# Two layers of a graph network and a mixture of experts: the first weights in two halves, and clears, a cast and filler matmuls moved at the start

## The chip, the cores and the metric

The kernel runs on one core of a Trainium2 chip. The metric is the device time of one launch in microseconds (us), the median of several runs. A profile is one further execution, taken by the hardware profiler; its times are counted from the start of its span.

## What is computed

x has 1250 rows of 1024 numbers; there are 40,000 edges, sorted by target. Everything is float32.

```python
def sage(h, W_self, W_neigh, b):        # twice, with a relu between
    agg = segment_sum(h[src], dst)      # sum over the edges that end in a row
    return h @ W_self + (agg * deg_inv[:, None]) @ W_neigh + b

x = x + sage2(relu(sage1(layernorm(x))))
t = layernorm(x)
logits = silu(t @ rw1 + rb1) @ rw2 + rb2          # 8 experts, the best 2 per row
w = softmax over the best 2
x = x + t + sum over experts of w[e] * (silu(t @ ew1[e] + eb1[e]) @ ew2[e] + eb2[e])
```

## The kernel before, in words

Rows go in ten blocks of 128 (the last has 98). The gather and sum over edges is done as a matrix product: a matrix C of counts (source row by target row, ten blocks of 128 x 1250) is built from one-hots, and a layer is C times (h times W_neigh), plus h times W_self. The kernel runs in stages: the start (rows in, layer norm, transposes into h0T), the self product of layer 1 with the counts in its gaps, the neighbour product and C times it, layer 2, the router, the experts.

The change lies in the start. What sets the order there:

- Loads (L150 to L159, L196). SyncE (SP) and ScalarE (ACT) each have a DMA queue. Blocks 0 and 1 of x come in two column halves each, one per queue (L153). Then SP loads the first quarter of W_self0, 1 MB, by `load_q` (L110), and blocks 4 and 5; ACT loads blocks 2 and 3 (L157) and src (L159), SP dst (L158). ACT also issues the load of the bias b0_p (L196), 1024 numbers of 4 bytes spread over 128 partitions, just after its first activation (L165), which also brings in the activation table. Blocks 6 to 9 are loaded later by `fetch_tokens` (L390), as the rows that they overwrite have been transposed. Each DMA raises a semaphore when it has landed; there are eight for these queues, taken in turn, so that a DMA waits on its queue until the one eight places earlier has landed.
- Clears of C (L356 to L365), before counts are added to it at L440. Ten blocks: 0, 1 and 5 to 7 by GpSimd (POOL), 2 and 3 by VectorE (DVE), 4 by ScalarE through `clear` (L363), 8 and 9 by ScalarE later, at L501.
- `layernorm_steps` (L311), a generator with three steps: statistics of the first half; statistics of the second half, their aggregate (L319) and the square root on ScalarE (L320); reciprocal (L322) and scaling (L323).
- The order written out by hand at L469 to L504 for VectorE, ScalarE and TensorE (`manual_schedule`): `pass_time` (L479) issues matmuls whose results nobody reads; `step` advances the layer norms of the blocks named; `turn_tokens` transposes a block on TensorE (L306) and copies it to h0T on ScalarE (L309); `self_unit` (L454) is one product of eight matmuls (L460) for a 128-column slice of the result and a chunk of rows, with the bias added on ScalarE (L464).
- `make_keys` (L209) works out each edge's place, `turn_keys` transposes the keys (L227, copied at L230), and after that the one-hots begin: `lane` (L189, a row 0 to 127 as float16, cast by `counted`, L186) is compared with the keys on POOL (L413) and ScalarE (L410, L411), `win` on VectorE (L418), and TensorE multiplies them (L421).
- `verdict` (L245) checks later whether this way of counting holds for the data; its first instruction is a memset of 960 numbers (L248).

What is not in the hand-written part is placed by a scheduler when the kernel is built; `keep_in_program_order` ties an instruction to its place in the program.

Of the kernel before, what the change touches and what calls it, by code (L numbers as in the profile page):

```python
# [12 lines left out]
F16 = mybir.dt.float16  # L13
# [8 lines left out]
P = 128  # L22
# [7 lines left out]
def kernel(  # L30
# [21 lines left out]
    nc = tc.nc  # L52
# [3 lines left out]
    KD = D // P  # L56
    KH = H // P
    HALF = D // 2
    QW = D // 4
# [14 lines left out]
    def blk(b):  # L74
        return slice(b * P, b * P + rows[b])
# [14 lines left out]
    WQ = KD * QW  # L90
# [3 lines left out]
    WW = L[:, NT + 4 * D :]  # L94

    def row_of(i):
        return SC[:, (i % 4) * D : (i % 4 + 1) * D]

    def first_row_of(i):

        return WW[:, WQ + (i - 4) * D : WQ + (i - 3) * D] if i in (4, 5) else row_of(i)

    turn = [0]

    def load_q(w, q):

        t = WW[:, turn[0] * WQ : (turn[0] + 1) * WQ].rearrange("p (k n) -> p k n", k=KD)
        turn[0] ^= 1
        tc.keep_in_program_order(
            nc.sync.dma_start(  # L110
                out=t, in_=w[:, q * QW : (q + 1) * QW].rearrange("(k p) n -> p k n", p=P)
            )
        )
        return t
# [35 lines left out]
    for b in range(2):  # L150
        for h, eng in enumerate((nc.sync, nc.scalar)):
            hs = slice(h * HALF, (h + 1) * HALF)
            eng.dma_start(out=row_of(b)[: rows[b], hs], in_=x[blk(b), hs])  # L153
    ws_first = load_q(w_self0, 0)
    for b in range(2, 6):
        eng = nc.scalar if b < 4 else nc.sync
        eng.dma_start(out=first_row_of(b)[: rows[b]], in_=x[blk(b), :])  # L157
    nc.sync.dma_start(out=dst_i, in_=dst.rearrange("(g n) -> g n", n=RE))  # L158
    nc.scalar.dma_start(out=src_i, in_=src.rearrange("(g n) -> g n", n=RE))  # L159
# [11 lines left out]
    def iota(shape, pattern, mult=0):  # L171

        n = 1
        for d in shape[1:]:
            n *= d
        ti = L[: shape[0], at_iota[0] : at_iota[0] + n].bitcast(I32)
        at_iota[0] += n
        assert at_iota[0] <= NT
        if len(shape) == 3:
            ti = ti.rearrange("p (a b) -> p a b", b=shape[2])  # L180
        nc.gpsimd.iota(ti, pattern=pattern, base=0, channel_multiplier=mult)
        return ti

    def counted(ti, name, dtype=F32):
        tf = const.tile(list(ti.shape), dtype, name=name)
        tc.keep_in_program_order(nc.vector.tensor_copy(tf, ti))  # L186
        return tf

    lane = counted(iota([P, P], [[1, P]]), "lane", F16)  # L189
    tiles_i = iota([P, NTILE], [[1, NTILE]])  # L190
    token_i = iota([P, NB], [[P, NB]], mult=1)
    own_row_i = iota([P, 1], [[0, 1]], mult=1)
# [6 lines left out]
    ext = base_i = keys = None  # L199
# [9 lines left out]
    def make_keys():  # L209

        nc.vector.tensor_reduce(ext[:, 0, :], dst_halves, AX.X, ALU.min)
        nc.vector.tensor_scalar(ext[:, 2, :], ext[:, 0, :], float(N - WIN), None, op0=ALU.min)
        nc.vector.tensor_scalar(hi_i, src_i, 7, None, op0=ALU.arith_shift_right)
        nc.vector.tensor_scalar(lo_i, src_i, P - 1, None, op0=ALU.bitwise_and)
        nc.vector.tensor_copy(hi_f, hi_i)
        nc.vector.tensor_copy(lo_f, lo_i)
        stt(key, hi_f, float(WIN), dst_f, op0=ALU.mult, op1=ALU.add)
        for i in range(2):
            part = key[:, i * EG : (i + 1) * EG]
            nc.vector.tensor_scalar(part, part, ext[:, 2, i : i + 1], None, op0=ALU.subtract)  # L220
# [11 lines left out]
    def turn_ranges():  # L232

        nc.vector.tensor_reduce(ext[:, 1, :], dst_halves, AX.X, ALU.max)
        for a in (2, 0, 1):
            pe = tpp.tile([P, 4, P], F32, name="tp")
            for i in range(2):
                nc.tensor.transpose(pe[:1, i, :R], ext[:, a, i : i + 1], ident[:R, :R])
            nc.vector.tensor_copy(
                gx[:, a, :].rearrange("o (r i) -> o i r", i=2), pe[:1, :2, :R]  # L240
            )
            if a == 2:
                nc.vector.tensor_copy(base_i, gx[:, 2, :])

    def verdict():  # L245

        bad = L[:1, 8480 : 8480 + 6 * NGR].rearrange("o (a g) -> o a g", a=6)
        nc.vector.memset(bad, -1.0)  # L248
        stt(bad[:, 0, :], hi_, float(1 - WIN), lo_, op0=ALU.add, op1=ALU.subtract)
        nc.vector.tensor_tensor(bad[:, 1, : NGR - 1], lo_[:, : NGR - 1], lo_[:, 1:], ALU.subtract)  # L250
        nc.vector.tensor_tensor(bad[:, 2, : NGR - 1], hi_[:, : NGR - 1], hi_[:, 1:], ALU.subtract)
        stt(
            bad[:, 3, : NGR - APART], hi_[:, : NGR - APART], 1.0, lo_[:, APART:],
            op0=ALU.add, op1=ALU.subtract,
        )
        nc.vector.tensor_scalar(bad[:, 4, :], hi_, float(1 - N), None, op0=ALU.add)
        nc.vector.tensor_scalar(bad[:, 5, :], lo_, -1.0, None, op0=ALU.mult)
        nc.vector.tensor_reduce(worst, bad.rearrange("o a g -> o (a g)"), AX.X, ALU.max)
        nc.vector.tensor_scalar(plain, worst, 0.0, None, op0=ALU.is_le)
# [51 lines left out]
    def layernorm_steps(o, t, m):  # L311

        st = small.tile([P, 2, 6], F32, name="st")
        mv = small.tile([P, 2], F32, name="mv")
        rs = small.tile([P, 1], F32, name="rs")
        nc.vector.bn_stats(st[:m, 0, :], t[:m, :HALF])
        yield
        nc.vector.bn_stats(st[:m, 1, :], t[:m, HALF:])
        nc.vector.bn_aggr(mv[:m], st[:m].rearrange("p a s -> p (a s)"))  # L319
        nc.scalar.activation(rs[:m], mv[:m, 1:2], AF.Sqrt, bias=eps[:m])  # L320
        yield
        nc.vector.reciprocal(rs[:m], rs[:m])  # L322
        nc.vector.tensor_scalar(  # L323
            o[:m], t[:m], mv[:m, 0:1], rs[:m], op0=ALU.subtract, op1=ALU.mult
        )
        yield
# [14 lines left out]
    def gnn_windows():  # L341
# [14 lines left out]
        for k in range(2):  # L356
            nc.gpsimd.memset(C[:, k, :].bitcast(F32), 0.0)
            nc.vector.memset(C[:, k + 2, :].bitcast(F32), 0.0)
        for k in range(5, 8):
            nc.gpsimd.memset(C[:, k, :].bitcast(F32), 0.0)  # L360

        def clear(k):
            nc.scalar.copy(C[:, k, :], none.to_broadcast([P, N]))  # L363

        clear(4)  # L365
        ones_r = cpool.tile([P, P], F32R, name="ones_r")
        nc.gpsimd.memset(ones_r.bitcast(F32), 1.0)

# [3 lines left out]

        yh = yp.tile([P, NB, QW], F32R, name="yh")
        yl = yp.tile([P, NB, QW], F32R, name="yl")
        nonlocal ext, base_i, keys
        ext = yp.tile([R, 3, 2], F32, name="ext")
        base_i = yp.tile([1, NGR], I32, name="base_i")

        keys = yp.tile([GP, 2, 2 * GC, R], F32, name="keys")
# [12 lines left out]
        def turn_tokens(b):  # L392
            put_transposed(h0T, 0, b, first_row_of(b), KD)
# [60 lines left out]
        def self_unit(w, d, c, halfway=None):  # L454
            c0, n = cchunks[c]
            ps = mm.tile([P, 512], F32, name="ps")
            for k in range(KD):
                if halfway is not None and k == KD // 2:
                    halfway()
                nc.tensor.matmul(  # L460
                    ps[:, :n], w[:, k, (d % 2) * P : (d % 2 + 1) * P], h0T[:, k, c0 : c0 + n],
                    start=(k == 0), stop=(k == KD - 1),
                )
            nc.scalar.activation(  # L464
                hT1[:, d, c0 : c0 + n], ps[:, :n], AF.Identity, bias=b0_p[:, d : d + 1]
            )


        with tc.manual_schedule(engines={ENG.DVE, ENG.Activation, ENG.PE}):  # L469
            norm = [layernorm_steps(first_row_of(b), first_row_of(b), P) for b in range(6)]  # L470

            def step(*bs):
                for b in bs:
                    next(norm[b])


            idle = mm.tile([P, 512], F32, name="ps")

            def pass_time(n):  # L479
                for _ in range(n):  # L480
                    nc.tensor.matmul(idle[:, :P], ident, ident, start=True, stop=True)

            pass_time(24)
            step(0, 0, 1, 0, 1)
            turn_tokens(0)
            step(1)
            turn_tokens(1)
            pass_time(4)
            step(2, 2, 3, 2, 3, 4, 3, 4)
            self_unit(ws_first, 0, 0)  # L490
            turn_tokens(2)
            step(5, 4, 5)
            self_unit(ws_first, 1, 0)
            step(5)
            turn_tokens(3)
            turn_tokens(4)
            turn_tokens(5)
            nc.vector.tensor_copy(dst_f, dst_i)
            make_keys()
            self_unit(ws_first, 0, 1, turn_keys)  # L500
            clear(8)  # L501
            clear(9)
            turn_ranges()
            self_unit(ws_first, 1, 1)  # L504
# [9 lines left out]
        some_groups(2)  # L514
        self_unit(ws_first, 1, 2)
        verdict()
        for q in range(1, 4):
            w_q = w_next
# [102 lines left out]
        for k in range(0, KB, 2):  # L621
            ks = slice(k, k + 2)
# [1100 lines left out]


    gnn_windows()
    ok = moe()
    with tc.If(ok == 0):
# [36 lines left out]
```

## Time and profile before

| | us |
|---|---|
| median of 3 runs | 1120.42 |
| lowest, highest | 1119.36, 6438.05 |
| the profiled execution | 1118.35 |
| its span, first to last instruction | 1116.6 |
| TensorE busy, of the span | 1089.5 (98%) |
| VectorE busy | 472.9 (42%) |
| POOL busy | 313.6 (28%) |
| ScalarE busy | 218.3 (20%) |

In a timeline a line has start, duration of the group, engine, line of the kernel, operation, what is written <- what is read, and in brackets the idle time of the engine before it with what ended it. SPq and ACTq are DMAs as they are issued on these queues, not their landing. In the chain of waits a line is start, length, and what the end of the kernel waited for in that stretch. In windows, after the stretch and its length, stand the busy times of TensorE, weight load, VectorE, ScalarE and POOL with the number of instructions, then TensorE's granted clock, the share of the 16 DMA engines and GB/s.

### The profile page before, as it was taken

To read this page: it belongs to the slowest core of one execution; us is meant where nothing else is said; L and a number is where in the kernel's file an instruction comes from. 1 tells how busy PE (TensorE), PEld (TensorE's weight loads), DVE (VectorE), ACT (ScalarE), POOL (GpSimd) and SP (SyncE) were. 2 spreads that over 40 slices of the span, in tenths; PEclk is the share of its full clock that TensorE was granted. 3 is DMA by queue.
4 is the path that set the end of the run, shared out by engine and by line. 5 is a ranking of instruction groups with operands and counts; after the bars stand their busy time and mean duration, and the time that the engine had idled before them with its cause. 6 is when DMAs were issued, how large, how long until landed. Compare 5 with 4: busy or idle time off the path is not lost.

```text
span 1116.6 us, 13639 instructions
## 1 busy us (share of the span) xinstructions
PE 1089.5 (98%) x4881; PEld 809.9 (73%) x4881; DVE 472.9 (42%) x1172; ACT 218.3 (20%) x511; POOL 313.6 (28%) x407
## 2 busy tenths in 40 slices
PE   8999999999999999999999999999999999999993
PEld 7556556888888888888888888887544577676761
DVE  8767777763121245342234142455522263222221
ACT  4522222101111101110010000023111133333331
POOL 2999898500000000022002211254000013232321
PEclk9999999999999999999999999999999999999997
DMA  8011011010100020033004270343960456677762
GB/s 260 12 39 40 1 38 39 2 38 1 38 1 1 1 76 19 1 114 126 22 1 154 96 269 7 105 171 147 334 207 1 160 180 180 183 182 192 192 172 47
DMA packets 62320, 107.37 MB, mean 96 GB/s; under 512 B 8906, under 2 KB 35690, under 8 KB 62240
## 3 DMA queue, kind: packets, MB, share of 16 engines
q1 hardware_dynamic: 51392, 79.69, 20.9%
q0 software_dynamic: 7056, 23.88, 9.2%
q10 hardware_dynamic: 3792, 2.79, 0.8%
q8 instruction: 43, 0.70, 0.3%
q14 instruction: 37, 0.30, 0.1%
HBM read 80.74 MB, written 27.42 MB: 97 GB/s over the span
## 4 chain that ended last, share of the span: by engine, by line
PE 74%; DMA 16%; DVE 4%; issue 3%; ACT 1%; POOL 1%; SPq 0%; POOLq 0%; ACTq 0%; DVEq 0%
DMA out_dram<-L 13%; PE ps L532 12%; PE ps L460 11%; PE psb L664 11%; PE ps L760 8%; PE ps L664 8%; PE ps L568 8%; PE ps L1230 4%; PE ps L1244 3%; PE cnt L421 3%; PE ps L1183 2%; DMA b_p<-in_L_gnn_b_dram 1%; DMA more<-in_L_gnn_W_self_dram 1%; DVE xw L140 1%; PE ps L1575 1%
## 5 line engine op out<-in xcount | busy, mean ns | idle before, releaser
L413 POOL TENSOR_SCALAR ol<-lane,keys 125x128 f16<-125x128 f16 x280 | 171.0, 628 | 31.8 <-ACT keys L230 22.3
L460 PE MATMUL ps<-h0T,L 128*128 128x498 f32 (+2 forms) x384 | 146.0, 514 | 0.2 <-ACT h0T L309 0.2
L532 PE MATMUL ps<-L,h0T 128*128 128x256 f32 (+1 forms) x640 | 142.2, 379 | 0.8 <-DVE yl L387 0.8
L756 POOL TENSOR_TENSOR L<-L 128x512 f32<-128x512 f32 (+1 forms) x20 | 28.2, 1417 | 393.5 <-DMA L<-in_x_dram 393.4
L532 PEld LDWEIGHTS ps<-L,h0T 128*128 128x128 f32 (+1 forms) x640 | 118.3, 187 | 19.0 <-DVE yl L387 1.1
L460 PEld LDWEIGHTS ps<-h0T,L 128*128 128x128 f32 x384 | 67.2, 190 | 38.7 <-issue 34.7
L418 DVE TENSOR_SCALAR oh<-win,keys 125x240 f16<-125x240 f16 x320 | 81.1, 307 | 29.7 <-PE cnt L421 28.0
L1575 PE MATMUL ps<-xw,L 128*128 x368 | 84.1, 380 | 0.7 <-issue 0.7
L1602 PE MATMUL ps<-xw,L 128*128 x184 | 82.8, 593 | 0.5 <-ACT L L1590 0.5
L568 PE MATMUL ps<-C,yh 128*128 128x256 f32 (+2 forms) x240 | 81.7, 355 | 0.0
L568 PE MATMUL ps<-C,yl 128*128 128x256 f32 (+2 forms) x240 | 81.4, 353 | 0.0
L760 PE MATMUL ps<-zh,C 128*128 128x512 f32 (+1 forms) x200 | 79.5, 398 | 0.0
L760 PE MATMUL ps<-zl,C 128*128 128x512 f32 (+1 forms) x200 | 78.6, 393 | 0.0
L1575 PEld LDWEIGHTS ps<-xw,L 128*128 128x128 f32 x368 | 68.0, 190 | 9.5 <-issue 1.4
L440 DVE TENSOR_TENSOR C<-C,cnt 128x240 f32 x160 | 64.4, 402 | 12.9 <-DVE C L440 1.3
L1608 POOL DMA_INDIRECT out_dram<-L x23 | 36.5, 1586 | 118.2 <-DVE L L1607 62.0
L1547 POOL DMA_INDIRECT L<-t_d,L x26 | 25.5, 980 | 143.7 <-DVE L L140 122.9
L1602 PEld LDWEIGHTS ps<-xw,L 128*128 128x128 f32 x184 | 34.9, 190 | 34.9 <-issue 32.3
L1607 DVE SCALAR_TENSOR_TENSOR L<-ps,L 128x512 f32<-128x512 f32 x46 | 34.5, 751 | 53.1 <-PE ps L1602 53.1
L664 PE MATMUL ps<-L 128*128 128x256 f32 x240 | 56.2, 379 | 0.0
L387 DVE TENSOR_TENSOR yl<-ps,yh 128x256 fp32r<-128x256 f32 (+1 forms) x40 | 16.9, 423 | 92.3 <-ACT yh L386 92.3
L421 PEld LDWEIGHTS <-ol 125*128 125x128 f16 x320 | 31.0, 97 | 34.3 <-POOL ol L413 16.5
(237 smaller groups left out, 1558.1 us busy)
## 6 DMA issues: line engine op xcount, KB each, us to landing
xw<-in_L_ffn_ew_dram SPq DMA_DIRECT2D x16, 1024.0 KB, 11.2
L<-in_L_ffn_eb_dram SPq DMA_DIRECT2D x23, 512.0 KB, 4.7
L<-in_x_dram SPq DMA_DIRECT2D x20, 256.0 KB, 2.6
v_d<-L SPq DMA_DIRECT2D x18, 256.0 KB, 2.0
xa<-v_d SPq DMA_DIRECT2D x18, 256.0 KB, 7.2
t_d<-L SPq DMA_DIRECT2D x9, 512.0 KB, 3.8
out_dram<-xa SPq DMA_DIRECT2D x9, 512.0 KB, 4.0
L<-in_L_gnn_W_self_dram SPq DMA_DIRECT2D x4, 1024.0 KB, 5.3
```

Source lines behind the costliest of these rows:

```text
L413: nc.gpsimd.tensor_scalar(ol[:, c, :], lane[:GP], k, None, op0=ALU.is_equal)
L418: nc.vector.tensor_scalar(oh, win[:GP], keys[:, 0, i * GC + c, r : r + 1], None, op0=ALU.is_equal)
L421: nc.tensor.matmul(ps[:, i, :GW], ol[:, i * GC + c, :], oh, start=(c == 0), stop=(c == GC - 1),)
L440: nc.vector.tensor_tensor(to, to.bitcast(F32), ps[:, i, :GW].rearrange("p (k w) -> p k w", k=NB), ALU.add,)
L460: nc.tensor.matmul(ps[:, :n], w[:, k, (d % 2) * P : (d % 2 + 1) * P], h0T[:, k, c0 : c0 + n], start=(k == 0), stop=(k == KD - 1),)
L532: nc.tensor.matmul(ps[:m, :QW], hT[:, k, blk(b)], w[:, k, :], start=(k == 0), stop=(k == KD - 1))
L568: nc.tensor.matmul(ps[:, :n], part[: rows[k], k, (d % 2) * P : (d % 2 + 1) * P], C[: rows[k], k, c0 : c0 + n], start=(k == 0 and part is y ...
L664: nc.tensor.matmul(ps, rows_of(k), w[:, k, :], start=(first and k == 0), stop=(k == KB - 1), skip_group_check=not first,)
L760: nc.tensor.matmul(ps[:m], C[: rows[k], k, blk(b)], part[: rows[k], k, :], start=(k == 0 and part is yh), stop=(k == NB - 1 and part is yl),)
L1230: nc.tensor.matmul(ps, a_[:, k, :], b_[:, k, :], start=(start and k == 0), stop=(stop and k == KB - 1),)
L1575: nc.tensor.matmul(ps[:, :H], xT[:, k, :], w1_all[:, ds(e, 1), k * H : (k + 1) * H], start=(k == 0), stop=(k == KD - 1),)
L1602: nc.tensor.matmul(ps, hT[:, q, :], w2_all[:, ds(e, 1), q * D + h * HALF : q * D + (h + 1) * HALF], start=(q == 0), stop=(q == KH - 1),)
```

## The change

- The first quarter of W_self0 is loaded in two halves of k (four of its eight 128-row blocks each), one on SP's queue and one on ACT's, in the place of one load on SP's queue.
- Of blocks 2 to 5 of x, even ones are on SP's queue and odd ones on ACT's; before, 2 and 3 were on ACT's, 4 and 5 on SP's.
- The cast of `lane` stands after `make_keys`, ahead of the transposes of the keys.
- The memset of the verdict is tied to its place in the program.
- Block 4 of C is cleared by POOL with 5 to 7, no longer by ScalarE.
- `pass_time` is 16 at the start, not 24, and 4 ahead of the first product are gone.

```diff
-    ws_first = load_q(w_self0, 0)
+
+    ws_first = WW[:, :WQ].rearrange("p (k n) -> p k n", k=KD)
+    turn[0] = 1
+    for h, eng in enumerate((nc.sync, nc.scalar)):
+        ks = slice(h * KD // 2, (h + 1) * KD // 2)
+        eng.dma_start(
+            out=ws_first[:, ks, :],
+            in_=w_self0[:, :QW].rearrange("(k p) n -> p k n", p=P)[:, ks, :],
+        )
     for b in range(2, 6):
-        eng = nc.scalar if b < 4 else nc.sync
+        eng = nc.scalar if b % 2 else nc.sync
         eng.dma_start(out=first_row_of(b)[: rows[b]], in_=x[blk(b), :])
...
-    lane = counted(iota([P, P], [[1, P]]), "lane", F16)
+    lane_i = iota([P, P], [[1, P]])
+    lane = None
...
-        nc.vector.memset(bad, -1.0)
+        tc.keep_in_program_order(nc.vector.memset(bad, -1.0))
...
-        for k in range(5, 8):
+        for k in range(4, 8):
             nc.gpsimd.memset(C[:, k, :].bitcast(F32), 0.0)
...
-        clear(4)
...
-            pass_time(24)
+            pass_time(16)
             step(0, 0, 1, 0, 1)
             turn_tokens(0)
             step(1)
             turn_tokens(1)
-            pass_time(4)
             step(2, 2, 3, 2, 3, 4, 3, 4)
...
             make_keys()
+            lane = counted(lane_i, "lane", F16)
             self_unit(ws_first, 0, 1, turn_keys)
```

The order in which the built program has ScalarE's instructions, with what each waits for in brackets, before and after:

```
before                                      after
x block 0, right half                       x block 0, right half
x block 1, right half                       x block 1, right half
x block 2                                   W_self0, second half of k
x block 3                                   x block 3
src [block 0, right half]                   x block 5 [block 0, right half]
table load                                  src [block 1, right half]
first activation                            table load
b0_p [block 1, right half]                  first activation
clear of C's block 4                        b0_p [W_self0, second half of k]
root of block 0                             root of block 0
```

More of the change, by code (lines that the diff above doesn't have):

```diff
@@ L374, in gnn_windows @@
         yl = yp.tile([P, NB, QW], F32R, name="yl")
-        nonlocal ext, base_i, keys
+        nonlocal ext, base_i, keys, lane
         ext = yp.tile([R, 3, 2], F32, name="ext")
```

## The prediction

> **What bounds the kernel now.** I read the page's busy shares first, then the chain of waits, then the timelines of ScalarE, VectorE and TensorE over the first 30 us, where every edit lies, and last the windows with the DMA rate.
>
> ```profile
> span 1116.6 us, 13639 instructions
> PE 1089.5 (98%) x4881; PEld 809.9 (73%) x4881; DVE 472.9 (42%) x1172; ACT 218.3 (20%) x511; POOL 313.6 (28%) x407
> ```
>
> TensorE leaves 27 us of 1116.6 idle. A change at the start can only move the point from which TensorE works without a break; what comes later keeps its length.
>
> ```profile
> 0.74 3.63 DMA L<-in_x_dram
> 5.81 13.03 DMA b_p<-in_L_gnn_b_dram
> 30.11 4.37 POOL ol L413 x4
> 34.94 6.72 PE ps L460 x16
> ```
>
> The chain of waits starts with rows of x, then follows one small transfer, the bias b0_p, issued on ScalarE's queue at 5.81 and landing at 18.84, and reaches TensorE, which then carries it. So two things set the start: block 0's way to TensorE, and the bias.
>
> ```profile
> 4.38 0.34 ACTq L159 DMA_DIRECT2D L<-in_src_dram  x1
> 4.75 1.28 ACT L165 ACT_TABLE_LOAD   x1 [4.75 <-DMA L<-in_x_dram]
> 5.81 0.40 ACTq L196 DMA_DIRECT2D b_p<-in_L_gnn_b_dram  x1
> 6.05 0.20 ACT L165 ACTIVATE rs<-eps 128x1 f32<-128x1 f32 x1
> 6.25 1.24 ACT L363 CAST C<-none 128x1250 fp32r<-128x1250 f32 x1
> 7.39 0.29 ACT L320 ACTIVATE rs<-mv,eps 128x1 f32<-128x1 f32 x1
> ```
>
> This is ScalarE. The order of instructions says which transfer each DMA on its queue waits for (a transfer takes over the semaphore of one eight places earlier): src waits for the second half of block 0, which lands at 4.36, and goes at 4.38; b0_p waits for the second half of block 1, which lands at 5.79, and goes at 5.81. The table load stands behind src and starts only at 4.75. A DMA that waits holds all of ScalarE behind it.
>
> ```profile
> 6.42 0.14 DVE L319 BATCH_NORM_AGGREGATE mv<-st 128x2 f32<-128x12 f32 x1
> 7.71 0.16 DVE L322 RECIPROCAL rs<-rs 128x1 f32<-128x1 f32 x1
> 7.91 0.81 DVE L323 TENSOR_SCALAR L<-L,mv,rs 128x1024 f32<-128x1024 f32 x1
> 8.78 1.09 PE L306 MATMUL tp<-ident,L 128*128 128x128 f32 x8 [0.22 <-DVE L L323]
> 11.05 1.07 PE L306 MATMUL tp<-ident,L 128*128 128x128 f32 x8 [1.17 <-ACT h0T L309]
> 12.84 3.62 PE L460 MATMUL ps<-h0T,L 128*128 128x256 f32 x16
> ```
>
> Block 0 goes root (7.39), reciprocal (7.71), scaling (7.91), transposes (8.78); block 1 follows 2.27 later by VectorE's fixed order; the first product starts at 12.84. From there to 34 us TensorE idles about 1.7 us in pieces, and from 35 to 430 hardly at all.
>
> **The change, part by part.** *Clear and casts.* Block 0's variance is there at 6.56, but its root waits until 7.39 for the 1.24 us clear of C's block 4 on ScalarE. The clear gone, it could run at 6.25: -1.14 if nothing takes its place. The memset of the verdict (0.86, at 5.63) and the lane cast (0.54, at 7.04) lie on VectorE before the reciprocal that waits for this root; they gain nothing more. Their new places: the memset among the counts near 51 us, where VectorE then waits 2.2 us for TensorE (0.86 if that cover went); the cast after the keys on VectorE, near 27.5, whose first readers, at 30 and later, wait for the keys' copies (0.54 if not). The clear as a fourth POOL memset: 3.33/3 = 1.11 us, ahead of the ones and the window iota (7.43), whose cast comes at 12.06; POOL then idles 22 us: 0 (1.11 if not). In all 0.
>
> *Filler.* 12 matmuls of 24 + 4 go. The first 8 end before 8.55, and the transposes wait for VectorE at 8.78; the last four end about when ScalarE's copy ends (11.71 + 1.07 = 12.78), and the product starts at 12.84: gain at most 0.06, taken as 0. The remaining 16 are 32 records: the trace has them start 213 ns apart to 4.5 us and 112 ns from there, so they end near 6.7.
>
> *ScalarE's queue, the term that decides.* It now holds block 0, block 1, half the weights, block 3, block 5, src, b0_p. One DMA more shifts whom each waits for: src now waits for block 1's half (5.79 instead of 4.36), so it goes at 5.81 to 6.15, the table load runs 6.18 to 7.46, the first activation to 7.68. b0_p now waits for the half of the weights on this queue, and behind b0_p stands block 0's root. When does that half land?
>
> ```profile
> 5.00:6.00 1.00, 1.00 (x11) 1.00 (x11) 0.86 (x2) 1.00 (x1) 1.00 (x2) 1.00 1.10 388
> 6.00:7.00 1.00, 1.00 (x11) 1.00 (x11) 1.00 (x3) 0.99 (x3) 1.00 (x2) 1.00 1.07 413
> 26.00:28.00 2.00, 2.00 (x6) 0.87 (x5) 2.00 (x7) 0.29 (x1) 0.00 (x0) 1.00 1.03 348
> ```
>
> The last number is GB/s. Two queues together moved 388 and 413; from 26 to 28 us one queue alone moved weights in 1 KB packets at 348. The Trainium skill (Trainium Kernel Development and Optimization, Key Constraints) speaks against the split: queues share the same 16 DMA engines, so a second one saves only time of issuing. Taken as a gain, the split would halve the weights' time to 0.5 MB / 0.36 = 1.5 us, landing near 7.3 and holding nothing (the table is loaded until 7.46). By the rule both halves run together: 1.05 MB at about 0.36 MB/us (1 KB packets) = 2.9 us from 5.2, when block 1's packets end, so 8.1, and 0.4 until the landing is reported (the spread of the landings in the trace is 0.3 to 0.6): 8.5. I take 8.5, since the windows show no sum above 413; ends 7.3 and 9.2. So b0_p goes at 8.5, takes 0.40, and the root starts at 8.94 instead of 7.39: **+1.55**.
>
> *Down to the product.* VectorE's order is fixed (block 1's second half stands behind block 0's scaling), so its chain moves whole: transposes of block 0 at 10.33, of block 1 at 12.60, product at 14.4. Blocks 2 and 3 had landed at 8.5 and 10.7, block 4 at 13.8; with the weights ahead, 2 and 3 land near 11.1 and 4 and 5 near 14; VectorE asks for block 2 at 12.4 and block 4 at 16.3. Hidden; if not, each us late is one lost on VectorE.
>
> *Bias.* It queues behind block 3, block 5 and src: 1.05 + 2.10 + 0.32 = 3.47 MB for both queues from 5.45 at 0.385 MB/us end at 14.5. Its 1024 packets of 4 B got some 125 per us beside 4 KB packets (12 to 17 us in the trace), 900 and more per us alone (rb1_p at 67 us). Blocks 8 and 9 (226 packets, 2.4 us) run beside it: some 300 packets, then 720 alone in 0.8: 17.7, reported near 18.3; bounds 16 and 14.5 + 1024/125 + 0.5 = 23.2. ScalarE asks for it after block 4's root, 17.52 + 1.55 = 19.1. So the stall that the page shows ("b_p", 1.40 us before L464) goes, but TensorE does not wait there: its second product runs until 20.79 + 1.55 = 22.3, and block 3's transposes need block 2's copies, over at 20.6. Nothing is won; nothing is lost while it lands before about 21.2.
>
> *Clock of TensorE.* From 6.7 to 10.3 it now idles 3.7 us. Row: an idle 1.17 us (9.87 to 11.05) left the 109 ns pace of transposes unchanged; after the last matmul, ending at 1100.19, the granted clock falls at 1103.60, 3.41 later. Rule: the Trainium skill (TensorE: Matmul & The Clock Gate, What's actually happening) says that a window of about 3.4 us spent idle halves the clock, and that the windows run freely. By the row nothing like it is shown in the middle of work: 0. By the rule a whole window lies in the gap with a chance of (3.7 - 3.4)/3.4 = 8%; then block 1's transposes (+0.8) and up to a further 1.2 us of products run at half pace: 0.8 to 2.0. I take 0.
>
> *Order of the counts.* From 34 to 230 us the schedule permutes counts and products; their number is the same. TensorE lost 1.1 us to POOL's one-hots in that stretch: bounds -0.5 and +1, taken as 0.
>
> *Sum.* -1.14 is not reached; 0 + 0 + 1.55 + 0 + 0 + 0 = +1.55. The profiled execution took 1118.35 (span 1116.6 + 1.75 around it), so 1119.9. The two ordinary runs shown, 1119.36 and 1120.42, lie 1.0 and 2.1 above it, mean 1.5: **1121.4**.
>
> **The rivals.**
> *A, the clock falls in the gap.* For: 3.7 against 3.41. Against: it barely fits. 1121.4 + 0.8 to 2.0 = 1122.2 to 1123.4.
> *B, the wait is short.* The weights' half lands before the table load is over; then the root starts at 7.68, +0.3: 1120.2. For: block 1's packets end a little earlier on SP's queue. Against: both halves share the engines.
> *C, the other side.* Nothing holds the root: the hardware lets it past the waiting DMAs, at 6.25, and TensorE works 1.14 earlier: 1118.7. It decides where the root starts before 7.39. Against: the table load waited 4.75 us behind src.
> *D, the bias is last again.* At 125 packets per us throughout it lands at 23.2, and block 2's copies with it; TensorE then stands up to 2 us at block 3, another 1 at blocks 4 and 5: up to 1124.4. It decides from a landing at 21.2.
>
> **How the numbers follow.** Forecast 0.55, A 0.13, B 0.12, C 0.10, D 0.10. Within the forecast, the landing (8.1 to 9.2) and the runs' own scatter of about 1 us give 1120 to 1122.8. The range leaves out half of C below (0.05 and the scatter's foot) and D's upper half with the scatter above: 1118.8 to 1124.2. The 2% about which a measurement of this kernel can tell from no change is 22 us, and no case reaches it: faster by more 0.01, within 0.98, slower by more 0.01.
>
> **What would show it.** The root of block 0 (L329 in the changed kernel) near 8.9, directly after the issue of b0_p near 8.5; the table load at 6.2; transposes of block 0 near 10.3; the first product near 14.4 at its old 3.6 us (longer: A); L472 without a wait for b_p (with one: D). The forecast is wrong if the root starts before 7.7, if b0_p goes with src, or if the shift at the first product is not there at 230 us.

## The result and the profile after

| | before | after |
|---|---|---|
| median of 20 runs each, us | 1119.07 | 1123.68 |
| lowest, highest, us | 1117.77, one run at 6438.05 | 1120.54, 1126.57 |
| ratio, 95% interval | | 1.0038, 1.0031 to 1.0045 |
| the profiled execution, us | 1118.35 | 1124.21 |
| its span, us | 1116.6 | 1122.4 |

The changed kernel is slower by 4.3 us (0.0038 of 1119). The forecast was 1121.4; the time lies inside the range of 1118.8 to 1124.2, near its upper end. It is a change of less than 2%, so "within 2%" came true; but its size is well measured, and it is nearly three times the +1.55 that the sum gave. Nothing here explains the one run at 6438.05; it moves neither the median nor the ratio.

The head of the page of the changed kernel:

```profile
span 1122.4 us, 13589 instructions
PE 1090.0 (97%) x4857; PEld 809.7 (72%) x4857; DVE 473.0 (42%) x1172; ACT 217.4 (19%) x510; POOL 313.7 (28%) x408
```

TensorE's busy time is the same within 0.5 us (1089.5 before); the span has grown by 5.8. So TensorE waits longer, and the chain of waits says where:

```profile
1.67 10.15 DMA L<-in_L_gnn_W_self_dram
...
11.85 0.40 ACTq L205
...
12.29 0.30 ACT rs L329
```

Before, the chain ran through the bias until 18.84. Now it starts with half of the first weights, issued on ScalarE's queue at 1.67 and landed at 11.82, then the issue of the bias, then block 0's root. The timeline of the changed kernel has the same stretch engine by engine:

```profile
5.85 0.34 ACTq L167 DMA_DIRECT2D L<-in_src_dram  x1
6.22 1.28 ACT L173 ACT_TABLE_LOAD   x1 [6.22 <-DMA L<-in_x_dram]
7.51 0.20 ACT L173 ACTIVATE rs<-eps 128x1 f32<-128x1 f32 x1
11.85 0.40 ACTq L205 DMA_DIRECT2D b_p<-in_L_gnn_b_dram  x1
12.29 0.29 ACT L329 ACTIVATE rs<-mv,eps 128x1 f32<-128x1 f32 x1 [4.58 <-DMA L<-in_L_gnn_W_self_dram]
12.82 0.81 DVE L332 TENSOR_SCALAR L<-L,mv,rs 128x1024 f32<-128x1024 f32 x1
13.69 1.97 PE L315 MATMUL tp<-ident,L 128*128 128x128 f32 x8 [5.47 <-DVE L L332]
17.71 3.74 PE L468 MATMUL ps<-h0T,L 128*128 128x256 f32 x16
```

ScalarE is ready at 7.71 and stands 4.58 us with nothing to do but wait for the weights' half. The root starts at 12.29 (7.39 before, +4.90), the first product at 17.71 (12.84 before, +4.87). The transposes take 1.97 in the place of 1.09, so the clock of TensorE has fallen too:

```profile
7.54:10.95 3.41, 0.67 (x6) 0.48 (x5) 0.00 (x0) 0.17 (x1) 1.33 (x3) 1.00 1.04 395
10.95:14.36 3.41, 0.67 (x3) 0.68 (x4) 1.67 (x4) 0.29 (x1) 0.00 (x0) 0.50 1.03 329
14.36:17.78 3.42, 3.12 (x16) 2.53 (x14) 2.99 (x8) 2.06 (x4) 0.00 (x0) 0.50 0.53 109
```

These are windows: the number before the DMA share is the granted clock, 0.50 from 10.95 to 17.78. What the start loses is carried on unchanged. The first matmul of three later stages, and the last matmul of all (us):

| | before | after | difference |
|---|---|---|---|
| first product (L460, L468 after) | 12.84 | 17.71 | +4.87 |
| its second run | 17.17 | 22.16 | +4.99 |
| product with C, layer 1 | 235.36 | 240.21 | +4.85 |
| product with C, layer 2 | 490.73 | 495.61 | +4.88 |
| last matmul | 1100.19 | 1106.05 | +5.86 |

The last microsecond comes in the router and expert stages. From the second product with C to the end the profile of before takes 609.5 us and that of after 610.4; those of the variants below whose granted clock does not fall there take 609.3 to 611.6, without order, so this is not put down to the change.

### The profile page after: what moved, and what is told of

Read it like the earlier page. It is cut to its first block, busy times and chain, and to the rows that moved or that the text cites. A ratio compares the mean times of both kernels' runs of the same rounds, so it can differ in the third digit from the quotient of the medians.

```text
span 1122.4 us, 13589 instructions
## 1 busy us (share of the span) xinstructions
PE 1090.0 (97%) x4857; PEld 809.7 (72%) x4857; DVE 473.0 (42%) x1172; ACT 217.4 (19%) x510; POOL 313.7 (28%) x408
## 4 chain that ended last, share of the span: by engine, by line
PE 75%; DMA 15%; issue 3%; DVE 3%; POOL 1%; ACT 1%; ACTq 0%; DVEq 0%; SPq 0%; POOLq 0%
PE ps L540 12%; DMA out_dram<-L 12%; PE ps L468 12%; PE psb L672 11%; PE ps L768 8%; PE ps L672 8%; PE ps L576 8%; PE ps L1238 4%; PE ps L1252 3%; PE cnt L429 3%; PE ps L1191 2%; DMA more<-in_L_gnn_W_self_dram 1%; DMA L<-in_L_gnn_W_self_dram 1%; PE tp L315 1%; DVE xw L140 1%
## 5 line engine op out<-in xcount | busy, mean ns | idle before, releaser
L468 PE MATMUL ps<-h0T,L 128*128 128x498 f32 (+2 forms) x384 | 147.0, 515 | 0.2 <-ACT h0T L318 0.2
L468 PEld LDWEIGHTS ps<-h0T,L 128*128 128x128 f32 x384 | 66.8, 190 | 38.7 <-issue 34.0
```

The source lines that it names most:

```text
L468: nc.tensor.matmul(ps[:, :n], w[:, k, (d % 2) * P : (d % 2 + 1) * P], h0T[:, k, c0 : c0 + n], start=(k == 0), stop=(k == KD - 1),)
```

## The experiments

My theory after the result: *the wait*. A DMA on ScalarE's queue that waits for an earlier one holds ScalarE, here for the weights' half; the half lands late because the two queues share the engines packet by packet. Rival *clock*: TensorE, idle for 5.5 us, fell to half pace, and that is the loss. Rival *rest*: clears, cast, memset and filler cost it. "The product with C" below is that of layer 1, which starts at 235.36 in the profile of before. "Before" and "after" below are the kernel before and the changed kernel; a ratio is always to the kernel before, with its 95% interval.

**1. After, with the bias on SP's queue.**

```diff
-    nc.scalar.dma_start(out=b0_p, ...)
+    nc.sync.dma_start(out=b0_p, ...)
```

> The changed kernel with one edit: the load of b0_p is issued on SP's queue, not on ScalarE's. Theory 1 (wait): block 0's root stands behind b0_p on ScalarE, which waits for ScalarE's half of the weights, landed at 11.82; without it the root follows the first activation, near 7.7, the transposes of block 0 start near 9.1, the first product between 12.5 and 13.1 (17.71 in the changed kernel, 12.84 before), and the time is that of before within 0.7 us, about 1119. Theory 2 (clock): TensorE's half clock from 10.95 to 17.78 costs the 4.6 us; it would go only as far as the idle gap goes. Theory 3 (bias late): b0_p, now behind dst, lands after 21.2 and the time stays above 1121.

Ratio 1.0008 (0.9997 to 1.0019), 14 runs. The timeline of this run:

```profile
7.67 0.28 ACT L329 ACTIVATE rs<-mv,eps 128x1 f32<-128x1 f32 x1
8.19 0.95 DVE L332 TENSOR_SCALAR L<-L,mv,rs 128x1024 f32<-128x1024 f32 x1
12.76 3.72 PE L468 MATMUL ps<-h0T,L 128*128 128x256 f32 x16 [0.24 <-ACT h0T L318]
```

The weights' half still lands late, at 11.50, and the bias still waits for it (issued at 11.52), but now on SP's queue, where no computing stands behind it. The root runs as soon as the first activation is over (7.67), and the product is back at 12.76. The product with C starts at 235.32. One word of the program takes back 0.0030 of the 0.0038, and the wait theory holds. The 0.9 us that are left lie a little above the 0.7 expected, and the interval includes none at all. They go with the granted clock: the four executions with a mean clock of 0.995 took 1118.8 us in the mean (fifteen of before with that clock 1118.5), the other ten 1121.1; in the profile it fell from 914.33 to 921.16.

**2. Before, with only the loads of the change** (the first hunk of the diff).

> The kernel before with the loads of the changed one alone (weights in two halves, rows of x even and odd); clears, cast, memset and filler as before. Theory 1 (wait): b0_p goes at 11.8, the clear of C's block 4 (1.24 us) and then the root stand behind it, root near 13.4, product near 18.7, time about 1125, that is 1 us above the changed kernel. Theory 2 (clock through less filler): with the 24 fillers the clock holds and the time is near 1120. If the clears and the cast were to blame: 1119.

Ratio 1.0051 (1.0034 to 1.0067), 6 runs. The timeline of this run:

```profile
10.86 0.40 ACTq L204 DMA_DIRECT2D b_p<-in_L_gnn_b_dram  x1
11.30 1.23 ACT L371 CAST C<-none 128x1250 fp32r<-128x1250 f32 x1 [3.59 <-DMA L<-in_L_gnn_W_self_dram]
12.44 0.29 ACT L328 ACTIVATE rs<-mv,eps 128x1 f32<-128x1 f32 x1
```

The half landed at 10.84; behind b0_p stood the old clear of C's block 4, and the root behind that. So the loads alone cost at least about as much as the whole change (the intervals overlap), and the rival *rest* falls. The first product came at 19.46, 6.62 late (the clock was 0.50 from 12.55 to 19.38), but the product with C only 5.06 late: here part of the loss was made up on the way.

**3. After, with the loads of before.**

```diff
-    for h, eng in enumerate((nc.sync, nc.scalar)):     # halves of k
+    ws_first = load_q(w_self0, 0)
...
-        eng = nc.scalar if b % 2 else nc.sync
+        eng = nc.scalar if b < 4 else nc.sync
```

> The changed kernel with the loads of before (one load of the weights on SP's queue, blocks 2 and 3 on ScalarE's); clears, cast, memset and filler as changed. Theory 1: the root runs at 6.3 (7.39 before), transposes of block 0 at 7.6, but the product waits for the weights, which land at 12.4 on that queue, and starts near 12.5 (12.84 before): time 1118.7, a gain of 0.4. If these edits brought their whole 1.14: 1117.9. Theory 2 (less filler costs clock): product longer than 3.6 us, time above 1120.

Ratio 1.0009 (0.9997 to 1.0021), 14 runs; the gain of 0.4 us that was expected is not seen. Here the root is early, at 6.27, as the missing clear allows. That gain is lost one instruction on:

```profile
4.03 4.41 POOL L361 MEMSET C<- 128x1250 f32 x4
6.27 0.29 ACT L321 ACTIVATE rs<-mv,eps 128x1 f32<-128x1 f32 x1
6.79 2.34 DVE L324 TENSOR_SCALAR L<-L,mv,rs 128x1024 f32<-128x1024 f32 x1
9.19 1.09 PE L307 MATMUL tp<-ident,L 128*128 128x128 f32 x8 [1.13 <-DVE L L324]
```

VectorE's scaling, 0.81 elsewhere, takes 2.34 us. POOL's four clears last until about 8.4 (4.03 + 4.41; its next instruction starts at 8.36), and 8.36 + 0.81 = 9.17, about when the scaling ends (9.13): it was held until they were over. Run 6, with one clear less, tests this. The Trainium skill (SBUF — State Buffer, SBUF: two separate sides) says that VectorE and GpSimd share a pair of ports under an exclusive lock, held for a whole instruction. This row agrees and gives it a price, 1.5 us: the scaling stood behind what was left of the third clear and the whole of the fourth. VectorE's statistics beside the same clears took their usual 0.7, so not every instruction is held. In the profile the clock fell too, from 201.78 to 205.19, and the product with C came 1.43 late.

**4. After, with more filler (38), so that TensorE doesn't idle.**

```diff
-            pass_time(16)
+            pass_time(38)
```

> The changed kernel with 38 fillers in place of 16, so that TensorE is busy until about 11 to 13 us and its clock does not fall. Theory 1 (wait): the root stays at 12.3, block 0's transposes take 1.1 us in place of 2.0, block 1's too, and the product starts 0.5 us earlier, near 17.1; time about 1123. Theory 2 (clock): the 4.6 us come back, time about 1119.5.

Ratio 1.0047 (1.0029 to 1.0064), 6 runs. The granted clock stayed at 1.00 at the start (from 6.93 to 204.90), and nothing was won:

```profile
11.31 0.29 ACT L329 ACTIVATE rs<-mv,eps 128x1 f32<-128x1 f32 x1 [2.99 <-DMA L<-in_L_gnn_W_self_dram]
12.71 1.09 PE L315 MATMUL tp<-ident,L 128*128 128x128 f32 x8
16.28 3.72 PE L468 MATMUL ps<-h0T,L 128*128 128x256 f32 x16 [0.24 <-ACT h0T L318]
```

The half landed at 10.85, and the product is 3.44 late at an unbroken clock; a fall from 204.90 to 208.31 came later, and the product with C is 4.88 late. The rival *clock* falls as the cause of the 4 us. What the clock cost in after is seen in the distance from root to product: 5.42 in after, 4.97 here, so 0.45 us.

**5. After, with the weights parted 5 to 3 blocks of k,** the smaller part on ScalarE's queue.

```diff
-        ks = slice(h * KD // 2, (h + 1) * KD // 2)
+        ks = slice(5, KD) if h else slice(0, 5)
```

> The changed kernel with the weights split five to three (640 packets of 1 KB on SP's queue, 384 on ScalarE's) in place of four to four. Theory (queues share by packet, and once SP's weights are through its packets are 4 KB): ScalarE's part is through before SP's, near 7.8 to 8.3, so b0_p goes at 8.3, the root of block 0 near 8.8 in place of 12.3, the product near 13.9, time about 1120.3. If ScalarE's queue is slow for another reason, its part lands after 10.5 and the time stays above 1122.

Ratio 1.0039 (1.0027 to 1.0050), 6 runs: no gain, though the wait became shorter as the theory says. The timeline of this run:

```profile
8.69 0.40 ACTq L205 DMA_DIRECT2D b_p<-in_L_gnn_b_dram  x1
9.13 0.29 ACT L329 ACTIVATE rs<-mv,eps 128x1 f32<-128x1 f32 x1 [1.30 <-DMA L<-in_L_gnn_W_self_dram]
14.55 5.51 PE L468 MATMUL ps<-h0T,L 128*128 128x256 f32 x16
```

The part landed at 8.66 and the product started at 14.55, 3.16 earlier than in after. But it ran for 5.51 us in the place of 3.6: the clock was 0.50 from 11.39 to 18.22, and the second product came 6.23 after the first (4.33 before). The fall, which cost little in after because TensorE had nothing to do then, hit full work here. The profile's product with C is 3.08 late.

**6. As 3, with C's block 4 cleared by ScalarE between later roots,** three clears on POOL.

```diff
-        for k in range(4, 8):
+        for k in range(5, 8):
...
-            step(2, 2, 3, 2, 3, 4, 3, 4)
+            step(2, 2, 3, 2)
+            clear(4)
+            step(3, 4, 3, 4)
```

> The run with the loads of before and the other edits (e3_old_loads), with one edit: block 4 of C is cleared by ScalarE again, between the roots of blocks 2 and 3, and POOL has three clears after the first two, not four. Theory (POOL's clears hold VectorE's scaling): POOL ends its clears at 7.36 in place of 8.44, and the scaling of block 0, which took 2.34 us from 6.79 to 9.13, ends near 8.0; transposes of block 0 at 8.1 (9.19), product at 12.4 when the weights have landed, time 1118.5 to 1119. If POOL has nothing to do with it, the scaling still ends at 9.1.

Ratio 1.0012 (1.0003 to 1.0021), 10 runs: slower than before, where the same or a small gain was expected. With POOL free sooner, the scaling takes 1.03, and block 0's transposes start at 8.10, against 8.78 before. Then:

```profile
12.80 5.38 PE L460 MATMUL ps<-h0T,L 128*128 128x256 f32 x16 [1.38 <-DMA L<-in_L_gnn_W_self_dram]
```

TensorE waits 1.38 us for the first weights, which in this order of loads land at 12.66 (12.42 in before). The clock, 0.50 from 13.30 to 16.71, then made the product 5.38 long in the place of 3.6, and the product with C came 1.15 late. An earlier block 0 alone can win at most 0.4 us: in the kernel before, the first product at 12.84 already stood just behind its weights.

**7. Bias on SP's queue, table loaded first, weights 5 to 3, blocks 4 and 7 of C cleared by ScalarE between later roots.**

> The changed kernel with what the runs point to: b0_p on SP's queue, the table load ahead of every DMA that waits, weights five to three, clears of C's blocks 4 and 7 by ScalarE between the roots of blocks 2, 3 and 4, so that POOL ends its clears at 6.25. Theory: root near 6.1, scaling over at 7.5, transposes of block 0 at 7.6 (8.78 before), the product near 11.2 (12.84 before): time 1.0 to 1.6 us below before, 1117.3 to 1118. If block 3's rows, late behind the weights (13.2), hold VectorE, half of that goes.

Ratio 1.0019 (1.0009 to 1.0029), 12 runs. A gain of 1.0 to 1.6 us was expected. The product starts at 11.01, 1.83 earlier than before, but then:

```profile
12.53 0.69 DVE L324 BATCH_NORM_STATS2 st<-L 128x6 f32<-128x512 f32 x1 [2.93 <-DMA L<-in_x_dram]
```

VectorE waits for block 2's rows, which land at 12.50, and the second product comes at 16.63, only 0.54 earlier. By the product with C the profile is 0.63 behind. What the weights win, the rows lose.

**8. After, with blocks 2 to 5 all on ScalarE's queue,** so that no rows compete with the weights' half from SP's queue.

```diff
-        eng = nc.scalar if b % 2 else nc.sync
+        eng = nc.scalar
```

> The changed kernel with blocks 2 to 5 all on ScalarE's queue behind its half of the weights, so that SP's queue has only dst behind its own half and no 4 KB packets run beside the weights. Theory (4 KB packets of SP's queue took the rate from ScalarE's half): the half lands near 8.6, as forecast, in place of 11.82; root near 9.1, product near 14.2, time about 1120.8. If the half is late for another reason it lands after 10.5.

Ratio 1.0036 (1.0022 to 1.0051), 4 runs. The timeline of this run:

```profile
9.89 0.40 ACTq L205 DMA_DIRECT2D b_p<-in_L_gnn_b_dram  x1
10.34 0.29 ACT L329 ACTIVATE rs<-mv,eps 128x1 f32<-128x1 f32 x1 [2.13 <-DMA L<-in_L_gnn_W_self_dram]
```

The half landed at 9.87 in the place of 11.82: the rows of the other queue held it back by 1 to 2 us (10.84 to 11.82 in the profiles where they run beside it). But 8.6 was expected, and 9.87 lies between that and the 10.5 of the rival: the rows are a large part of the delay and not all of it. The clock fell twice (10.15 to 16.98 and 204.71 to 208.12), and the product with C was 4.53 late.

**9. As 5, with filler (28, and the 4 back),** to keep the clock up.

```diff
-            pass_time(16)
+            pass_time(28)
...
+            pass_time(4)
             step(2, 2, 3, 2, 3, 4, 3, 4)
```

> The changed kernel with the weights parted 5 to 3 blocks of k, as before in one run, but with TensorE's filler made longer (28 at the start, and the 4 ahead of the first product back), so that it doesn't idle while the root waits. Theory (the landing of ScalarE's part holds the root, and in the 5:3 run the fallen clock took back what the earlier landing gave): root 9.1, transposes of block 0 at 10.5, first product 14.1 to 14.6, no half clock before 25 us, second product 4.4 later at 18.5 to 19, ratio to the kernel before 1.0010 to 1.0020. Rival (the clock was not what took it back): the second product again 6.2 after the first, or the ratio stays at 1.0039.

Ratio 1.0039 (1.0027 to 1.0051), 12 runs from 1120.99 to 1126.39: above what was expected, and the same 1.0039 as without the filler, which was one sign of the rival. The other sign did not come: in the profile the clock stayed up, and the second product came 4.33 after the first:

```profile
10.12 0.29 ACT L329 ACTIVATE rs<-mv,eps 128x1 f32<-128x1 f32 x1 [2.41 <-DMA L<-in_L_gnn_W_self_dram]
15.57 3.62 PE L468 MATMUL ps<-h0T,L 128*128 128x256 f32 x16
```

But the same part of the weights landed at 9.65, not at 8.66: 15 of the 16 DMA engines had reported by 8.72, the last one 0.93 later, and the wait is for all. The profile lost 2.8 us (root +2.73, product +2.73, product with C +2.80). The timed runs lost 4.4, and the clock of each run tells them apart: five with a mean granted clock of 0.994 or more took 1121.3 us in the mean, 2.3 above the runs of before at such a clock, and the seven below it 1124.1. Why it falls in more runs here than in before, and where, was not seen in a profile and stays open.

**10. Three blocks of rows first.** Blocks 0, 1 and 2 in halves on both queues ahead of the weights' halves, the table first, bias and src on SP's queue, clears of C's blocks 4 and 7 between later roots, filler 14 and 2.

> Blocks 0, 1 and 2 of x in halves on both queues ahead of the weights' two halves, the table loaded first, the bias on SP's queue, the clears of C's blocks 4 and 7 on ScalarE between later roots. Theory (what is left of the start is the rows' and the weights' arrival, and a change there is carried to the end one to one): root 6.0 to 6.3, first product 11.0 to 12.5, no wait of VectorE for block 2, second product 15.5 to 17, time 0.5 to 1.6 us below the kernel before (ratio 0.9986 to 0.9996). Rival (the engines' sum of bytes sets it, so a row that comes earlier makes the weights late by as much): the first product waits for weights until 12.8 or later and the ratio is 1.000 to 1.002.

Ratio 1.0001 (0.9991 to 1.0011), 12 runs. The root was expected at 6.0 to 6.3 and came at 7.70:

```profile
4.34 3.32 ACTq L168 DMA_DIRECT2D L<-in_x_dram  x2
7.70 0.29 ACT L328 ACTIVATE rs<-mv,eps 128x1 f32<-128x1 f32 x1 [4.06 <-DMA L<-in_x_dram]
```

The first line holds the issues of blocks 3 and 5. Block 5's takes over the semaphore of block 2's right half, waits until that lands at 7.30, and the root stands behind it: the same mechanism again, with another transfer, that I had built in without seeing it. The first product came at 13.95, not at 11.0 to 12.5: the weights had landed at 11.31, so it did not wait for them as the rival had it, but the late root and a clock of 0.50 from 11.05 to 14.46 held it. The ratio is the rival's.

**11. As 1, with the filler of before (24 and 4).**

> The changed kernel with the bias on SP's queue and the filler of the kernel before (24 and 4). If the 0.0008 that the run with the bias alone on SP's queue stayed above the kernel before came from the clock falling at the start for want of filler: ratio 0.9997 to 1.0003. If it comes from the changed order of the counts near 200 us: 1.0005 to 1.0012, with the half clock near 201 to 208 in the profile. First product 12.8 to 13.1 either way.

Ratio 1.0019 (1.0005 to 1.0033), 12 runs; the point lies above both of the narrow bands that were expected, and the interval overlaps that of run 1. The filler is no help. Block 1's transposes start at 11.44 (11.45 in run 1), but the first product at 13.24 (12.76): 0.48 later, because the four matmuls of `pass_time(4)` still run when the copy that the product waits for is over:

```profile
12.34 1.06 PE L489 MATMUL ps<-ident 128*128 128x128 f32 x8
13.24 3.62 PE L468 MATMUL ps<-h0T,L 128*128 128x256 f32 x16
```

**12. As 10, with block 5 on SP's queue.**

```diff
-        eng = nc.scalar if b % 2 else nc.sync
+        eng = nc.scalar if b < 4 else nc.sync
```

> As the run with three blocks of rows first, but block 5 goes on SP's queue instead of ScalarE's. In that run block 5's transfer stood ahead of block 0's root on ScalarE's queue, waited there for block 2's right half (landed 7.3) and kept the root until 7.70. Theory (a transfer that waits on ScalarE's queue holds what stands behind it): the root at 6.0 to 6.3, transposes of block 0 at 7.5 to 8, those of block 1 at 9.7 to 10.2, first product 11.3 to 12.0 (it needs block 1's first copy and the weights, which landed at 11.3), second product 15.6 to 16.6, C's product 0.5 to 1.5 us earlier than in the kernel before, ratio 0.9980 to 0.9995. Rival (the root waited for something else): root again after 7.5, ratio 0.9993 to 1.001.

Ratio 1.0001 (0.9989 to 1.0014), 12 runs. Of the timeline:

```profile
5.81 0.29 ACT L328 ACTIVATE rs<-mv,eps 128x1 f32<-128x1 f32 x1 [2.17 <-DVE mv L327]
10.91 3.68 PE L467 MATMUL ps<-h0T,L 128*128 128x256 f32 x16
14.18 0.69 DVE L324 BATCH_NORM_STATS2 st<-L 128x6 f32<-128x512 f32 x1 [3.28 <-DMA L<-in_x_dram]
16.08 1.06 PE L314 MATMUL tp<-ident,L 128*128 128x128 f32 x8 [1.49 <-issue]
```

The root comes 1.89 earlier than in run 10, for a transfer moved from one queue to the other, and the first product starts at 10.91, 1.93 ahead of before. But block 3's rows land only at 14.16; VectorE waits 3.28 us for them, and in its fixed order block 2's scaling stands behind (15.16). TensorE waits for that, the second product comes at 16.98 (17.17 before), and at the product with C the profile is 0.78 behind. The theory of the root is right and the forecast of a gain wrong: rows and first weights together fill the DMA engines until about 14 us (their share in windows of 2 us is 0.93 to 1.10 from 2 to 14), and in the orders tried here one of them was always late. None of the twelve was faster than the kernel before.

## Why the prediction was right and wrong

**The mechanism was right.** Two queues, one more DMA, so b0_p waits for the weights' half and holds the root: run 1 against after, and run 12 against run 10, show it, each with one transfer moved to the other queue and no other edit. The table load was to start at 6.2 and did (6.22). The shift was to be whole at 230 us, and it is (+4.87 at the first product, +4.85 at 235). The bias was not to be late, and L472 has no wait for it; it landed at 16.11, earlier than the 18.3 worked out.

**The size was wrong in one term,** the landing of ScalarE's half: 8.5 in the sum, with ends 7.3 and 9.2, and 11.82 in the profile (10.84 to 11.82 in five profiles with this order of loads). Packets of the two queues in the changed kernel that ended in each half microsecond, counted in the trace (those of 4 bytes left out):

```
from us    SP's queue                     ScalarE's queue
5.0        103 x 1 KB, 4 x 2 KB           43 x 2 KB
5.5        148 x 1 KB                     41 x 1 KB
6.0         95 x 1 KB                     88 x 1 KB
6.5         85 x 1 KB                     87 x 1 KB
7.0         61 x 1 KB, 6 x 4 KB           79 x 1 KB
7.5         20 x 1 KB, 24 x 4 KB          52 x 1 KB
8.0         38 x 4 KB                     36 x 1 KB
8.5         41 x 4 KB                     45 x 1 KB
9.0         33 x 4 KB                     43 x 1 KB
9.5         40 x 4 KB                     20 x 1 KB, 5 x 4 KB
```

The step said: "By the rule both halves run together: 1.05 MB at about 0.36 MB/us". Two things in it fail. The halves don't start together: SP's block 1 was over first, and by 6.0 SP's half had sent 251 of its 512 packets, ScalarE's 41. And they don't compete with each other alone. SP's half is sent by about 8.0; then block 2 follows on SP's queue in packets of 4 KB, and the queues get about equal numbers of packets: 36, 45, 43 of ScalarE's beside 38, 41, 33 of SP's. At equal numbers, a queue of 1 KB packets beside one of 4 KB gets a fifth of the bytes. ScalarE's half had 165 packets left at 8.0, where the rate that I used would have taken 0.5 us; all but 21 were over by 10.0, and the last at 10.99. The Trainium skill (DMA: Bandwidth & Descriptors, Queues, rings and completion order) says that each engine goes round the queues packet by packet, by which it means a bundle of several descriptors; the records counted here are single pieces of 1 or 4 KB. The equal numbers agree with taking turns; how many pieces go at a turn is not shown. It was this page that bore on the step, not the one on shared engines that I weighed. The report came 0.8 after the last packet, where I had allowed 0.4. Run 8, in which SP's queue carries no rows behind its half, parts the error of 3.3 us: its last packet ended at 8.95, where the sum had 8.1, so 0.85 of it is there without the rows (the late start among it); from 8.95 to 10.99, 2.0, go with the rows (the last packet ended at 10.16 to 10.99 in the five profiles of this order); and 0.4 is the report.

**The other terms.**

- *Filler, 0 (at most 0.06)*: it was worth more. In before the product started right behind `pass_time(4)`, 12.84; without it it starts as soon as block 1's first copy is there. Runs 1 and 11 put that at 0.48. The row to compare was the first of the two copies, not the last.
- *Clock, 0*: rival A's fall came, and not for the reason that I weighed. The gap itself was reckoned wrongly: the filler was to end near 6.7, but the granted clock rose only at 7.54 (at 4.51 in before), its matmuls stood 213 ns apart until then, and it ended at 8.21; TensorE then idled 5.5 us, to 13.69. And I asked whether a whole window of 3.41 us fits into the gap. In after, the fall at 10.95 followed a stretch of 3.41 us in which TensorE was idle for 2.74. It cost 0.45 (root to product 5.42 against 4.97 in run 4), which the filler's gain cancels. Root +4.90, filler -0.48 and clock +0.45 make +4.87, what the product shows.
- *Clear removed, -1.14, not reached*: right for this change, and rival C would have been wrong about its size. Run 3 reaches the early root (6.27), and POOL's added clear holds VectorE until 8.4; run 6 removes that too, and the weights hold the product.
- *POOL's fourth clear, 0 (1.11 if not)*: 0 only while the root is late. Run 3 shows 1.5.
- *Order of the counts, 0 (-0.5 to +1)*: from the second product to the product with C, after changed by -0.14, and the other profiles with an unbroken clock there by -1.6 (run 2) to +1.2 (run 7), which is wider than the bounds.

**What was luck.** That the time lies in the range owes something to two errors. The upper part of the range was there for the rivals: D, the late bias, did not happen, and A's fall came but was cancelled by the filler. And the base of the sum was too high: 1118.35 and 1.5 from two ordinary runs make 1119.9, where twenty runs have the median 1119.07. With that base the forecast would have been 1120.6, 3.1 below the time measured.

## What to carry to other kernels

When a DMA is added to a queue, list for each later DMA which earlier one it now waits for, and what computing stands behind it on the issuing engine. Put waiting transfers on an engine that has nothing else to do. Reckon a transfer's landing from the packets, not the bytes: beside another queue with packets four times as large, it got a fifth of the bytes here, and the slowest of the engines decides.

## What the runs showed of the hardware

The granted clock changes on a grid: its stretches in the record of after are 3.41, 6.83 and 1092.27 us, and 1092.27 is 320 times 3.4133 (the longest of before, 1099.09, is 322 times that). It falls after much less than a window without work. In run 3 it fell for 3.41 us at 201.78:

```profile
198.37:201.78 3.41, 1.87 (x11) 0.99 (x10) 3.25 (x12) 0.77 (x2) 3.41 (x7) 1.00 0.01 2
201.78:205.19 3.41, 3.41 (x12) 2.68 (x10) 3.34 (x14) 0.40 (x1) 3.41 (x6) 0.50 0.02 5
```

In the first stretch TensorE worked for 1.87 us, and the two waits in it, of 0.67 and 0.83 us, were enough. Falls followed stretches with 1.53 to 3.41 us idle in the runs above; in runs 1 and 9 stretches with 1.5 us idle, and in run 3 one with 1.64 (from 1102.90), stayed without one. The way back asks for more work: full clock returned only after a stretch with at most 0.36 us idle, and after one with 0.65 (run 1, from 914.33) it stayed at half. So some falls last 3.41 us and others 6.83. The Trainium skill (TensorE: Matmul & The Clock Gate, What's actually happening) speaks of at least one idle window of about 3.4 us; here the measurement decides, and less than half a window idle can do. The grid lies differently in each execution (the first rise comes at 4.51 to 7.75), so the same waits can bring a fall in one and none in another; each 3.41 us at half clock costs up to 1.7 us, an estimate from the length of the stretch. The clock fell near 201 to 208 us in runs 3, 4 and 8, near 669 in run 3 and near 914 to 921 in runs 1 and 11, not in the others. Runs of one kernel differ by 2 to 8 us, and the slow ones among them mostly have the lower mean clock: in the twenty runs of after, the seven at 0.992 took 1122.3 us in the mean and the two at 0.988 took 1126.5. One stretch of 3.41 us at half lowers the mean by 0.0015 (1.7 of 1120). That fits, but no run held the clock fixed, so it is not shown as the cause.
